# Later column starts and another split of hand-carried groups (28 / 27 / 5 in place of 29 / 28 / 4) in a graph-network layer on one Trainium2 core

## The chip, the cores and the metric

The kernel runs on one core of a Trainium2 chip. A core has five engines, each with an instruction queue of its own that runs in order: TensorE (PE, with its weight loads listed apart as PEld), VectorE (DVE), ScalarE (ACT), GpSimd (POOL) and SyncE (SP, which in this kernel issues DMAs). The engines wait for one another through semaphores only. The metric is device time in microseconds of one execution. Three runs of the kernel took 3390.92, 3395.1 and 3396.24 us, so the median is 3395.1 us.

## The reference

One layer of message passing with a gated update, over N = 12,500 nodes of 128 features and E = 400,000 edges of 32 features. The edges arrive sorted by their destination `dst`; their sources `src` are random.

```python
h = relu(layernorm(x))                                  # x is 12500 x 128
m = relu(concat(h[src], h[dst], ea) @ w1 + b1) @ w2 + b2
agg = segment_sum(m, dst, 12500)
gi, gh = agg @ w_ih + b_ih, h @ w_hh + b_hh
r = sigmoid(gi_r + gh_r);  z = sigmoid(gi_z + gh_z)
n = tanh(gi_n + r * gh_n)
out = x + (1 - z) * n + z * h
```

The costly part is `h[src]`: for each of 400,000 edges a random row of 128 floats.

## The kernel before

**Tables.** A first part computes `h` and keeps it turned round in fast memory (`hT_all`, a column of 128 features for each node). It writes to device memory A = h @ w1[0:128] (the source's part of the edge product) and B = h @ w1[128:256] + b1 (the destination's).

**Pairs and units.** The edges are 3125 tiles of 128. Eight tiles make a *pair* k (391 pairs; the first has five tiles), and half a pair is a *unit* u (782 units, k = u // 2). The main loop goes through the units. For pair k, TensorE forms the destination and edge parts of eight tiles (`pre`, line 683, weights times `L` and `RW`), VectorE adds the eight gathered rows of A and applies the relu in one instruction (`add`, line 713), and TensorE sums the result by destination (`seg`, line 739). Work is pipelined by hand: in unit u the program puts `pre` of unit u+3, `add` of unit u+2 and `seg` of unit u, so pair k's add stands in unit 2k-1. Every 14 pairs a block of nodes is finished by `node`, with gate products, activations and an output row block.

**Four ways to bring the source rows of a pair.**

- *POOL.* For most pairs GpSimd issues eight indirect DMAs (`gather`, line 163), each of which fetches 128 rows of A into one of 11 buffers `G`. The buffers are a ring: a pair takes the buffer of the pair gathered eleven pairs before it, and its first gather waits until that pair's add has read the buffer. The first nine pairs (RAW) are gathered from x itself, and their norm is computed on the spot, before A is complete.
- *ScalarE* ("act"). For some pairs ScalarE copies 1024 columns of `hT_all` one by one into `HE_act` (line 979); it reads 16 column numbers at a time into registers (line 961). TensorE multiplies them by w1a (line 694), and ScalarE applies the relu (line 725) in place of VectorE's add.
- *VectorE* ("dve"). The same on VectorE, two columns per instruction (512 instructions of line 986 a pair, and eight repacking copies of line 991), with 32 numbers per register load.
- *SyncE* ("sp"). SP issues 1024 DMAs of one row of A each (line 968) into `G_sp`, with 32 numbers per register load (line 961). VectorE then adds them as for a gathered pair. There is one `G_sp` buffer.

Such a hand-carried pair is called a group below. Which pairs are groups, and in which units an engine works on each, comes from two tables:

```python
SPREAD = {"dve": 28, "act": 29, "sp": 4}     # lines 56-57
START = {"dve": 10, "act": 2, "sp": 24}
...
for m, n in SPREAD.items():
    lo, hi = START[m] // 2 + 2, NP - {"dve": 5, "act": 3, "sp": 12}[m]
    for i in range(n):
        k = lo + int((i + 1) * (hi - lo) / n)
        while k in mode:
            k += 1
...
        end = 2 * k - (8 if m == "sp" else 4)
        jobs.setdefault(start, []).append((m, k, end - start))
        start = end if m != "sp" else 2 * k + 2
```

Each engine has a column of groups, one behind the other. A group's 1024 copies or DMAs are cut into steps (`STEP`: 4 or 8 of them) and `run_jobs` lays these steps evenly over the units from the group's start to its end, four times in each unit, between the other instructions of that engine's queue. The order is therefore fixed when the program is written; what the engines do with it in time is decided by the queues and semaphores.

**SP's queue** also carries, in the same order, the loads that all pairs need. `fetch` (lines 574 and 577) brings `L` for two pairs; it stands in unit 2k, for k even, for pairs k+6 and k+7, and waits until TensorE has read the buffer of pair k. `window_rows` (line 613) brings two row blocks `RW` of B in unit 2k for pair k+4, whose `pre` stands in unit 2k+5, five units on. At each block end come the output store (854), two stores of a new piece of B (258 and 260; the next `window_rows` waits until they have landed) and the next block's load of x (755).

**The end.** The last pair (390) is added in two halves, and `last_node` finishes the last block behind it.

Of the kernel before, what the change touches and what calls it, by code (L numbers as in the profile page):

```python
# [52 lines left out]
PIECE = 128  # L53
STEP = {"act": 4, "dve": 8, "sp": 4}
ROW = 4 * D
SPREAD = {"dve": 28, "act": 29, "sp": 4}
START = {"dve": 10, "act": 2, "sp": 24}
NR = 12672

H_AT = 16512  # L60
# [3 lines left out]
def tile_gnn(ctx: ExitStack, tc: tile.TileContext, x, src, srcT, dstT, dstP, eaT, eaP, w1, b1, w2T, b2,  # L64
# [25 lines left out]

    mode, order = {}, {m: [] for m in SPREAD}
# [3 lines that stand above are left out]
# [447 lines left out]
    def check_windows():  # L542
        m = const.tile([128, 2], F32, name="lim1")
        nc.vector.tensor_reduce(m[:, 0:1], lim[:, 0, :], AX.X, ALU.max)
        nc.vector.tensor_reduce(m[:, 1:2], lim[:, 1, :], AX.X, ALU.min)
        bad = const.tile([128, 2], F32, name="bad")
        nc.vector.tensor_scalar(bad[:, 0:1], m[:, 0:1], float(V - 1), None, op0=ALU.is_gt)
        nc.vector.tensor_scalar(bad[:, 1:2], m[:, 1:2], 0.0, None, op0=ALU.is_lt)
        one = const.tile([128, 1], F32, name="one")
        nc.vector.tensor_tensor(one, bad[:, 0:1], bad[:, 1:2], op=ALU.max)  # L550
        pm = SEGB[1][:, 384:512]
        nc.tensor.transpose(pm[0:1, :128], one, ident)
        f = const.tile([1, 8], F32, name="flags")
        nc.vector.tensor_reduce(f[:, 0:1], pm[0:1, :128], AX.X, ALU.max)
        nc.vector.tensor_reduce(f[:, 1:2], off_f, AX.XY, ALU.max)
        nc.vector.tensor_reduce(f[:, 2:3], step_f, AX.X, ALU.max)
        nc.vector.tensor_scalar(f[:, 3:4], blk_f[:, NB - 1:NB], float(N - BLOCKS[-1][2]), None,
                                op0=ALU.not_equal)
        nc.vector.tensor_copy(f[:, 4:5], beyond)
        nc.vector.tensor_reduce(f[:, 6:7], f[:, 0:5], AX.X, ALU.max)  # L560
        nc.vector.tensor_copy(flag, f[:, 6:7])
# [435 lines left out]
    for m, kl in order.items():  # L997
        start = START[m]
        for k in kl:
# [75 lines left out]
    for u in range(NU):  # L1075
        k, h = divmod(u, 2)
        gathers(u)
        if h == 0:
# [14 lines left out]
            if k == NP - 20:  # L1093
                check_windows()
        if u == min(START.values()) - 2:
            nc.vector.tensor_scalar(at[:NJ, :], at[:NJ, :], place_of[:, 0:1], place_of[:, 1:2],
# [192 lines left out]
```

## Time and profile before

| | us |
|---|---|
| median of three runs | 3395.1 |
| the profiled execution, whole | 3398.46 |
| its span, from first to last instruction | 3396.4 |

| engine | busy | what fills it |
|---|---|---|
| ACT | 3183.8 us, 94% | 29,696 column copies |
| POOL | 2536.6 us, 75% | 2637 gathers; between two of them about 0.3 us of issue, which is not counted as busy |
| PE | 2410.5 us, 71% | `pre`, `seg`, gates |
| DVE | 2254.8 us, 66% | adds, column copies; register loads in between are not counted as busy |

The granted TensorE clock was 0.795 in the mean. The profile was taken on an execution 3.4 us longer than the median. "Idle" in a row is the time in which an engine stood still just before the instructions of that row, with what ended it; "issue" means that it waited for nothing that the profile shows, which here is mostly register loads (DVE, ACT) or the engine's own overhead between two DMAs (POOL). SP's instructions never count as busy; they are seen in the order of time (the timeline) and in the waits of SP's own queue, written SPq.

### The profile page before, as it was taken

Reading aid. Unit: us, or ns where it says so; the run is one execution under the profiler, and the core shown is the slowest. Engines: PE = TensorE matmul, PEld = TensorE weight load, DVE = VectorE, ACT = ScalarE, POOL = GpSimd, SP = SyncE. Lnnn points to the kernel's source line nnn. Section 1 sums busy time; section 2 is a strip of 40 time slices with the busy share of each in tenths; the row PEclk is TensorE's granted clock in tenths of the full one; section 3 lists DMA queues with packets and bytes.
Section 4 is the critical chain, followed back from the end, with each engine's and each line's share of the span. In section 5 each row is a group of like instructions: output and inputs, shape, how many; then the busy total and the mean of one; then the engine's idle time right before and its main releaser. Section 6 shows DMA issues by size and latency. Waiting matters only on the chain. (4 is left out here: it accounts for less than half of the span.)

```text
span 3396.4 us, 92978 instructions
## 1 busy us (share of the span) xinstructions
PE 2410.5 (71%) x13145; PEld 1547.7 (46%) x13145; DVE 2254.8 (66%) x16792; ACT 3183.8 (94%) x30083; POOL 2536.6 (75%) x2646
## 2 busy tenths in 40 slices
PE   7568767776677677677767776776676577767767
PEld 7445434444444344444444443454444344444445
DVE  8566667667666676676666666666666666666665
ACT  7699999999999999899999999999998999999995
POOL 7767777777777777777777777777777777777774
PEclk9777778877878788787778778777777887778878
DMA  6333444434434444343344343443443433444432
GB/s 214 97 85 87 101 99 95 99 94 106 95 96 98 99 97 96 95 103 95 92 100 97 92 100 94 102 93 97 97 102 87 101 94 94 100 100 96 94 94 62
DMA packets 194428, 334.67 MB, mean 99 GB/s; under 512 B 68293, under 2 KB 115972, under 8 KB 193809
## 3 DMA queue, kind: packets, MB, share of 16 engines
q0 software_dynamic: 84384, 172.99, 22.8%
q1 hardware_dynamic: 109281, 155.66, 17.2%
q14 instruction: 510, 4.18, 0.4%
q8 instruction: 109, 1.79, 0.2%
q10 hardware_dynamic: 144, 0.07, 0.0%
HBM read 308.21 MB, written 20.24 MB: 97 GB/s over the span
## 5 line engine op out<-in xcount | busy, mean ns | idle before, releaser
L163 POOL DMA_INDIRECT G<-A,src_i x2568 | 2469.5, 962 | 803.0 <-issue 761.5
L979 ACT COPY HE_act<-hT_all 128x4 uint8 x29696 | 2993.9, 189 | 52.9 <-issue 27.2
L986 DVE SCALAR_TENSOR_TENSOR both<-hT_all 128x4 uint16 x14336 | 1214.1, 154 | 990.4 <-issue 980.6
L683 PE MATMUL pre<-RW,L 128*128 128x256 f32 x3128 | 1130.2, 487 | 217.0 <-DVE RB L713 200.4
L683 PEld LDWEIGHTS pre<-RW,L 128*128 128x128 f32 x3128 | 662.5, 236 | 500.2 <-DVE RB L713 216.2
L739 PE MATMUL seg<-RB,OH 128*32 128x129 f32 x6250 | 609.4, 326 | 308.1 <-DVE RB L713 238.9
L739 PEld LDWEIGHTS seg<-RB,OH 128*32 128x32 f32 x6250 | 334.8, 126 | 802.2 <-DVE RB L713 460.3
L713 DVE CUSTOM_DVE_ANT_0 RB<-pre,G 128x1024 f32<-128x1024 f32 x322 | 389.4, 1210 | 26.0 <-PE pre L683 21.6
L734 PE MATMUL seg<-zrow 1*128 1x129 bf16 x196 | 45.9, 234 | 215.0 <-DVE OH L633 212.7
L586 DVE TENSOR_SCALAR L<-L,node_of 64x512 f32<-64x512 int32 x382 | 188.7, 494 | 10.7 <-DMA L<-in_dstP 10.7
L633 DVE TENSOR_TENSOR OH<-dloc,seg 128x512 f32<-128x512 f16 (+1 forms) x198 | 132.2, 668 | 0.0
L765 PE MATMUL nd<-spot,sums 128*128 128x40 f32 x782 | 114.5, 316 | 4.8 <-DVE sums L748 4.7
L765 PEld LDWEIGHTS nd<-spot,sums 128*128 128x128 f32 x782 | 109.8, 226 | 14.4 <-issue 8.8
L991 DVE COPY HE_dve<-both 128x512 uint8<-128x512 uint8 x224 | 102.4, 457 | 7.7
L848 PE MATMUL nd<-ident,gt 128*128 128x128 f32 (+2 forms) x112 | 28.5, 400 | 98.0 <-DVE gt L844 88.0
L694 PEld LDWEIGHTS pre<-w1a,HE_act 128*128 128x128 f32 x464 | 82.0, 221 | 9.5
L244 PE MATMUL nd<-w1b,hT_all 128*128 128x128 f32 x224 | 45.5, 346 | 56.5 <-DVE xb L850 56.5
L694 PEld LDWEIGHTS pre<-w1a,HE_dve 128*128 128x128 f32 x448 | 78.8, 220 | 9.2
L163 POOL DMA_INDIRECT G<-in_x,src_i x69 | 65.7, 952 | 21.9 <-issue 20.7
L694 PE MATMUL pre<-w1a,HE_act 128*128 128x128 f32 x464 | 80.5, 302 | 0.0
L725 ACT ACTIVATE RB<-pre 128x1024 f32<-128x1024 f32 x66 | 66.8, 1013 | 13.2 <-PE pre L694 13.2
L694 PE MATMUL pre<-w1a,HE_dve 128*128 128x128 f32 x448 | 77.7, 302 | 0.0
(177 smaller groups left out, 1374.9 us busy)
## 6 DMA issues: line engine op xcount, KB each, us to landing
G_sp<-A SPq DMA_DIRECT2D x4096, 0.5 KB
L<-in_dstP SPq DMA_DIRECT2D x195, 256.0 KB
L<-in_eaP SPq DMA_DIRECT2D x195, 256.0 KB
G<-A,src_i POOLq DMA_INDIRECT x2568, 2.6
RW<-B SPq DMA_DIRECT2D x782, 16.0 KB
xb<-in_x SPq DMA_DIRECT2D x26, 256.0 KB
out<-xb SPq DMA_DIRECT2D x26, 256.0 KB
xs<-in_x SPq DMA_DIRECT2D x11, 512.0 KB
```

The costliest lines, as they stand in the source:

```text
L163: fetched = nc.gpsimd.indirect_dma_start(out=G[k][:, j, a, :], out_offset=None, in_=table, in_offset=bass.IndirectOffsetOnAxis(ap=src_i[c] ...
L586: nc.vector.tensor_scalar(o, i, node_of[:, k:k + 1], None, op0=ALU.is_equal)
L633: nc.vector.tensor_tensor(p, dloc[:, e0:e1, None].to_broadcast(shape), row[:, None, :].to_broadcast(shape), op=ALU.is_equal)
L683: nc.tensor.matmul(p[:, 2 * i:2 * i + 2, :], Ls[k // QP][:, c0:c0 + 128], RW[k % 4], start=True, stop=not raw)
L694: nc.tensor.matmul(p[:, 2 * i + a, :], cols, w1a, start=False, stop=n + 1 == len(l) or l[n + 1][1] != j)
L713: made = nc.vector._custom_dve(TENSOR_ADD_SAT, out=o, in0=p, in1=G[k].rearrange("p j a f -> p (j a) f")[:, c, :], s0=float("inf"), s1=0.0)
L725: nc.scalar.activation(o, p, AF.Relu)
L739: nc.tensor.matmul(p[r0:r0 + V, :D + 1], OH[k][:, a * GRP + j, :], RB[k % 2][:, 2 * j + a, :D + 1], start=False, stop=all(b != a for _, _, ...
L765: nc.tensor.matmul(p[:, bass.ds(offs[i], V + SHIFT)], sums[:, slot(b, i), :D], spot[:, i % 2, :], start=False, stop=i == len(offs) - 1)
L979: nc.scalar.copy(he[:, e * 4:e * 4 + 4], column(v))
L986: nc.vector.scalar_tensor_tensor(both[:, (e0 % PIECE + i) // 2, :], column(vals[i + 1]), 256.0, column(vals[i]), op0=ALU.mult, op1=ALU.add)
L991: nc.vector.tensor_copy(he[:, p0 * 4:(p0 + PIECE) * 4].rearrange("p (n c b) -> p n c b", c=2, b=4), both.bitcast(U8).rearrange("p n (b c) ...
```

## The change

```diff
-SPREAD = {"dve": 28, "act": 29, "sp": 4}
-START = {"dve": 10, "act": 2, "sp": 24}
+SPREAD = {"dve": 27, "act": 28, "sp": 5}
+START = {"dve": 14, "act": 4, "sp": 24}
```

By the formula above this gives:

| | before | after |
|---|---|---|
| groups in all | 61 | 60 |
| pairs that POOL gathers | 330 (2637 gathers) | 331 (2645 gathers) |
| ScalarE's column | 29 groups in units 2 to 772; pairs 16, 29, 42, 56 ... 374, 388 | 28 groups in units 4 to 772; pairs 17, 31, 45, 58 ... 374, 388 |
| units per ScalarE group | 26, now and then 28 | first 26, then 28, now and then 26 |
| VectorE's column | 28 groups in units 10 to 768; pairs 20, 34, 47 ... 372, 386 | 27 groups in units 14 to 768; pairs 22, 36, 50 ... 372, 386 |
| units per VectorE group | 26 and 28 by turns | first 26, then 28 |
| SP's column | 4 groups (pairs 105, 197, 287, 379) of 178, 174, 170, 174 units, in units 24 to 750 | 5 groups (pairs 87, 160, 233, 306, 379) of 142, 136, 136, 136, 136 units, in units 24 to 750 |

Between two SP groups lie ten units (five pairs) without SP rows, in both kernels. One instruction on VectorE that turns the node numbers of all groups into addresses (line 1096) moves from unit 0 to unit 2, since its place is two units ahead of the first column. Nothing else changes: the arithmetic, the ring of 11 buffers, and all other loads and their places stay.

## The prediction

> **What bounds the kernel now.** I read the page first, then the waits of POOL, then POOL's and VectorE's timelines against each other.
>
> ```profile
> span 3396.4 us, 92978 instructions
> L163 POOL DMA_INDIRECT G<-A,src_i x2568 | 2469.5, 962 | 803.0 <-issue 761.5
> L979 ACT COPY HE_act<-hT_all 128x4 uint8 x29696 | 2993.9, 189 | 52.9 <-issue 27.2
> L986 DVE SCALAR_TENSOR_TENSOR both<-hT_all 128x4 uint16 x14336 | 1214.1, 154 | 990.4 <-issue 980.6
> L991 DVE COPY HE_dve<-both 128x512 uint8<-128x512 uint8 x224 | 102.4, 457 | 7.7
> ```
>
> Three engines look full. ScalarE's copies alone take 2994 us. VectorE's column takes 1214 us of copies and 981 us of issue (register loads). POOL's gathers and their issue fill almost everything. The first question is which of them waits. From 200 us on, POOL's waits were:
>
> ```profile
> POOL G L163 <- issue: 739.3, 2422, 0.3
> POOL G L163 <- DVE RB L713: 16.4, 14, 7.7
> POOL G L163 <- DVE both L986: 8.5, 28, 0.3
> ```
> ```profile
> 400.00:3200.00 2800.00, 2125.73 (x2210) 0.79 0.41 97
> ```
>
> POOL waited for others hardly at all; from 400 to 3200 us (POOL's busy time in that window) it issued 2210 gathers in 2800 us, 1.267 us each. So it runs at its own pace, 10.1 us a pair. POOL's timeline shows where it stood still, and the last gathers of pairs 36, 376 and 390; VectorE's shows the adds of those three pairs (counted off in program order):
>
> ```profile
> 198.18 0.95 POOL L163 DMA_INDIRECT G<-A,src_i  x1 [1.72 <-PE misc L666]
> 215.62 0.95 POOL L163 DMA_INDIRECT G<-A,src_i  x1 [7.75 <-DVE RB L713]
> 316.97 0.94 POOL L163 DMA_INDIRECT G<-A,src_i  x1 [0.93 <-DVE RB L713]
> 331.02 0.94 POOL L163 DMA_INDIRECT G<-A,src_i  x1 [4.36 <-DVE RB L713]
> 350.10 0.95 POOL L163 DMA_INDIRECT G<-A,src_i  x1 [0.30 <-issue]
> 3250.00 0.95 POOL L163 DMA_INDIRECT G<-A,src_i  x1 [0.30 <-issue]
> 3361.32 0.95 POOL L163 DMA_INDIRECT G<-A,src_i  x1 [0.31 <-DMA G<-A,src_i]
> ```
> ```profile
> 445.36 1.21 DVE L713 CUSTOM_DVE_ANT_0 RB<-pre,G 128x1024 f32<-128x1024 f32 x1
> 3280.55 1.23 DVE L713 CUSTOM_DVE_ANT_0 RB<-pre,G 128x1024 f32<-128x1024 f32 x1 [0.63 <-PE pre L683]
> 3376.27 1.29 DVE L713 CUSTOM_DVE_ANT_0 RB<-pre,G 128x512 f32<-128x512 f32 x2 [3.12 <-PE pre L683]
> ```
>
> The *lag* from the end of a pair's last gather to its add is 445.36 - 351.05 = 94.3 us at pair 36, 29.6 us at 376 and 14.0 us at 390. Early on the ring is full and the consumers (VectorE, ScalarE, TensorE) hold POOL back. After 331 us POOL never waits again, and the consumers eat up the backlog: from pair 36 to 376 they take (3280.55 - 445.36) / 340 = 8.34 us a pair, while POOL needs (3250.95 - 351.05) / 340 = 8.53 us for each pair of the sequence, groups included. So the consumers set the end, but POOL is only 14 us behind as a bound. A change that frees the consumers soon runs into POOL.
>
> **The change, part by part.** (1) *One more pair for POOL.* Eight gathers at 1.267 us: +10.1 us on POOL's end. Its pace becomes 8.53 + 10.1 / 391 = 8.56 us a pair.
>
> ```profile
> L163 POOL DMA_INDIRECT G<-A,src_i x2568: 942/947/1624, 92.9 to 3361.3; - x198
> ```
>
> A rule of the Trainium skill bears on this price (SBUF — State Buffer, "Who interferes with whom"): a VectorE copy in a two-port mode locks GpSimd out of a shared port while it runs, and gathers issued by GpSimd need that port for their descriptors. By the rule, eight repacking copies of line 991 fewer, at 457 ns, could give POOL back up to 3.7 us, and the sum would be that much lower. The gather's median of 947 ns (least, median, most in the row above) and its mean of 962 leave about 40 us over all gathers for every such disturbance, so the trace allows the rule a small part only; I add nothing for it.
>
> (2) *ScalarE and VectorE have one group less.* ScalarE's copies take 2993.9 / 29696 = 0.101 us each, 103 us a group; spread over 387 pairs that frees 0.27 us a pair. On VectorE a group is (1214.1 + 980.6 + 102.4) / 28 = 82 us, or 0.21 us a pair. If they alone set the pace, the consumers come to 8.34 - 0.21 = 8.13 us a pair, well under POOL's 8.56.
>
> (3) *SP has one group more, and each is denser.* This is the part with a price.
>
> ```profile
> L968 SPq DMA_DIRECT2D G_sp<-A x4096: 224/228/760, 240.8 to 3267.5; - x196
> L961 SPq TENSOR_LOAD <-at x128: 1872/2148/2357, 238.4 to 3247.9; - x128
> ```
> ```profile
> 1119.13 3.91 SPq L968 DMA_DIRECT2D G_sp<-A  x12
> 1123.14 0.81 SPq L613 DMA_DIRECT2D RW<-B  x2
> 1124.05 6.04 SPq L968 DMA_DIRECT2D G_sp<-A  x12
> 1130.35 0.40 SPq L854 DMA_DIRECT2D out<-xb  x1
> 1132.29 0.42 SPq L258 DMA_DIRECT2D B<-xb  x1
> 1132.77 0.52 SPq L260 DMA_DIRECT2D B<-xb  x1
> 1136.60 0.90 SPq L613 DMA_DIRECT2D RW<-B  x2
> ```
> ```profile
> L968 SPq DMA_DIRECT2D G_sp<-A x840: 224/228/706, 1101.3 to 1699.4; - x168
> ```
> ```profile
> SPq L574 <- PE pre L683: 71.9, 17, 14.9
> SPq L613 <- PE pre L683: 16.0, 6, 9.1
> SPq L613 <- DMA B<-xb: 14.7, 5, 3.2
> SPq L574 <- PE pre L694: 3.7, 2, 1.9
> ```
>
> (The first two rows are the whole run's, then come a stretch of SP's timeline, the SP rows between 1100 and 1700 us, and SP's waits in those 600 us.) Twelve rows occupy SP for 1123.14 - 1119.13 = 4.01 us, 0.334 us each, and a register load adds about 2.2 us (the stretch of 6.04 us holds one): a group costs 1024 x 0.334 + 32 x 2.2 = 412 us. In the 600 us, waiting for TensorE (71.9 + 16.0 + 3.7 = 92 us) is SP's whole slack. It worked 508 us, 840 / 1024 x 412 = 338 of them on rows and 170 on everything else, landings of B included; at 8.34 us a pair that is 72 pairs, so 2.36 us a pair. After the change a group lies in 136 units, 68 pairs: 412 + 68 x 2.36 = 572 us, which is 8.42 us a pair, or, with 420 us for a group (the rows vary), 8.53. That is over the 8.13 of the other consumers and just under POOL's 8.56. SP becomes nearly full.
>
> What covers SP's lateness: `RW` is asked for five units ahead, 5 x 4.07 = 20.3 us at 8.13 us a pair. The profile has no landing time for RW; nearest is a gather's, which is
>
> ```profile
> DMA to landing us min/median/max: 2.5/2.7/5.5
> ```
>
> and at a block end SP bunches about 6 us (1130.35 to 1136.60 above). That leaves C = 20.3 - 2.7 - 6 = 12 us that SP may fall behind before TensorE waits; the bounds are 0 (a late SP costs at once) and 17 (no bunching). Between two groups SP has five pairs with little to do, 5 x (8.13 - 2.36) = 29 us, and starts anew.
>
> One cycle of 73 pairs then takes the consumers 420 + 68 x 2.36 + 5 x 8.13 - C = 621 - C, against POOL's 73 x 8.56 = 625. The lag is 94 us at pair 36, falls by 0.43 x 47 = 20 until the end of the first, longer group (pair 83), and then by 4 + C in each of four cycles: at pair 376 it is 94 - 20 - 16 - 4C, 10 us for C = 12, 58 for C = 0, nothing for C = 17. The last fifteen pairs took 29.6 - 14.0 = 15.6 us off it, and their groups are the same as before. So for C = 12 the add of the last pair waits for its rows alone, 2.7 us behind the start of the last gather, in place of 14.9: -12.2 us. For C = 0 the lag ends at 42, +28 us. I take -11, since stretches with a burst of node work leave a few us.
>
> The Trainium skill has a rule that speaks against this part (DMA: Bandwidth & Descriptors, "Rules for kernel authors" and "Anatomy of one DMA"): small transfers are mostly overhead, about 2 us fixed for each. Paid one after the other by SP, 1024 rows would be 2048 us by that page's figure, no group would fit, and the kernel would take over 10 ms. The trace disagrees on that reading: 4096 rows went out in 3027 us beside everything else. The fixed time is overlapped, and I give the rule no chance of its own here.
>
> (4) *Later starts.* POOL's four early waits above, less 0.3 us of issue each, are 1.4 + 7.45 + 0.6 + 4.1 = 13.5 us of standing still because the buffer's consumer was late. Two units without copies take 2 x 39.4 x 0.101 = 8 us out of ScalarE's queue ahead of the first two waits; but ScalarE was not full there,
>
> ```profile
> 100.00:200.00 100.00, 61.92 (x372) 50.68 (x374) 61.30 (x352) 77.29 (x509) 72.61 (x77) 0.76 0.34 85
> 200.00:300.00 100.00, 74.79 (x379) 45.49 (x378) 64.52 (x516) 99.15 (x951) 69.98 (x75) 0.76 0.34 84
> ```
>
> (the fourth busy time is ScalarE's: 77 of the first 100 us, 99 of the next), so about half of it reaches the add: 4 us. The last two waits (4.7 us) should go: by then the columns are two to four units behind, and one group (pair 17) stands before pair 21 where there were two (16 and 20), so POOL asks for that buffer one pair later. I take -8 us; bounds 0 and -13.5. A loss is excluded while SP's rows, which start in the same unit, have the cover above.
>
> VectorE's address instruction in unit 2 rather than 0 costs nothing: one instruction, still two units ahead of its reader. The two pairs that change from a ScalarE relu to a VectorE add are 1.2 us of VectorE each, inside its 82 us.
>
> *Sum:* 10.1 - 8 - 11 = -8.9 us. The profiled execution, 3398.46, becomes 3389.6; the median of the runs stands 3.4 us lower, so 3386.
>
> **The rivals.**
>
> *SP runs out of cover (the other side).* Place: TensorE's `pre`, waiting for RW or VectorE's L. Price: each us of C that is missing adds 4 us at pair 376. It decides from C under 8 us: there the end's lag is over 14 - 2.1 us and outweighs the gains. With C = 4 the lag ends at 42 - 16 = 26, +12 in place of -11: 10.1 - 8 + 12 = +14, 3409; with C = 0 it is +30, 3425. For it: 8.42 to 8.53 us a pair leaves SP almost nothing within a group, and B's landing (14.7 us in 600) can't be hidden. Against it: SP was waiting for TensorE 15% of the time, and in the whole run TensorE waited for RW in three places only:
>
> ```profile
> PE pre L683 <- DMA RW<-B: 16.6, 3, 11.3
> ```
>
> *The gains at both ends are small, and POOL's pair eats them.* The early waits stay (0) while the end still tightens: 10.1 - 11 = -1, 3394. Or the early waits go and the end's lag stays at 14 because node work, not groups, makes it: 10.1 - 8 = +2, 3397. For it: ScalarE's idle 23 us in the window with the two early waits; against it: the lag falls steadily through the run, so it is a backlog and not a fixed delay.
>
> *The consumers were all that counted* (the change does more than I allow): the end falls by VectorE's 82 us, 3313. Against it: POOL's 2645 x 1.267 us alone is 3351, with 34 us from its last gather to the span's end behind it. I give it nothing.
>
> **How the numbers follow.** Forecast 0.45; SP out of cover 0.33; small gains 0.22. The forecast's own range, from all early waits gone and C = 17 (10.1 - 13.5 - 12, -15) to C = 9 (-5), is 3380 to 3390. To reach 8 in 10 the range takes in the small gains and the rival up to about C = 2: 3379 to 3418. A difference under 0.2%, 7 us, can't be told from none here. Faster than that is the forecast; no change is the small gains; slower is SP out of cover: 0.45, 0.22, 0.33.
>
> **What would show it.** Right: POOL's waits on DVE RB after 200 us fall under 9 us; its last gather starts near 3363; the add of the last pair waits for the landing, and in the second half of the run VectorE's adds are held up by gathers rather than by TensorE. SP's waits for TensorE shrink from 92 us in 600 to some 20. Wrong: TensorE or VectorE waiting for RW or L in SP's groups, with a lag that no longer falls; POOL waiting on the ring beyond 400 us; or SP rows that cost other than 0.33 us.

## Result, and the profile after

The changed kernel takes 3381.91 us (median of five runs, 3379.55 to 3383.87), the kernel before 3396.24 us in five runs; the ratio is 0.9955, 95% interval 0.9941 to 0.9969. The forecast was 3386, with a range of its own of 3380 to 3390. The profiled execution has a span of 3382.1 us against 3396.4, so the two traces differ by 14.3 us. From the page of the changed kernel (the columns as on the page before: busy, mean ns of one, idle just before with what ended it):

```profile
span 3382.1 us, 93395 instructions
...
L163 POOL DMA_INDIRECT G<-A,src_i x2576 | 2475.8, 961 | 790.4 <-issue 761.2
L979 ACT COPY HE_act<-hT_all 128x4 uint8 x28672 | 2889.0, 189 | 52.9 <-issue 29.1
L986 DVE SCALAR_TENSOR_TENSOR both<-hT_all 128x4 uint16 x13824 | 1174.3, 154 | 930.3 <-issue 925.6
L683 PE MATMUL pre<-RW,L 128*128 128x256 f32 x3128 | 1136.1, 489 | 461.3 <-DMA RW<-B 237.7
...
L713 DVE CUSTOM_DVE_ANT_0 RB<-pre,G 128x1024 f32<-128x1024 f32 x323 | 391.1, 1211 | 70.9 <-DMA G<-A,src_i 56.5
```

Two of these rows read quite differently from before. TensorE's `pre` now waits 238 us for RW, which SP brings (before: 16.6). VectorE's add now waits for gathered rows, 56.5 us (before: not at all). The second is the mark of POOL as the bound. POOL's waits from 200 us on, its last gathers of pairs 37, 261, 370, 376 and 390 (36 is a VectorE group now, so 37 stands for it), and the adds of the same pairs:

```profile
POOL G L163 <- issue: 738.0, 2420, 0.3
POOL G L163 <- DVE both L986: 7.6, 25, 0.3
POOL G L163 <- DVE RB L713: 5.2, 17, 0.3
```
```profile
345.79 0.94 POOL L163 DMA_INDIRECT G<-A,src_i  x1 [0.30 <-issue]
...
2261.59 0.95 POOL L163 DMA_INDIRECT G<-A,src_i  x1 [0.30 <-issue]
...
3203.85 0.94 POOL L163 DMA_INDIRECT G<-A,src_i  x1 [0.30 <-issue]
...
3244.44 0.95 POOL L163 DMA_INDIRECT G<-A,src_i  x1 [0.31 <-issue]
...
3354.97 0.94 POOL L163 DMA_INDIRECT G<-A,src_i  x1 [0.30 <-issue]
```
```profile
441.81 1.21 DVE L713 CUSTOM_DVE_ANT_0 RB<-pre,G 128x1024 f32<-128x1024 f32 x1
...
2272.34 1.21 DVE L713 CUSTOM_DVE_ANT_0 RB<-pre,G 128x1024 f32<-128x1024 f32 x1
...
3210.39 1.22 DVE L713 CUSTOM_DVE_ANT_0 RB<-pre,G 128x1024 f32<-128x1024 f32 x1
...
3265.06 1.23 DVE L713 CUSTOM_DVE_ANT_0 RB<-pre,G 128x1024 f32<-128x1024 f32 x1 [0.33 <-PE pre L683]
...
3361.10 1.29 DVE L713 CUSTOM_DVE_ANT_0 RB<-pre,G 128x512 f32<-128x512 f32 x2 [3.15 <-PE pre L683]
```

No wait of POOL on a buffer is longer than its usual 0.3 us any more: the early waits are gone. The lag is 95 us at pair 37 (before: 94 at pair 36), 10 at 261, 6 at 370, 20 at 376 and 5 at 390. So the consumers have eaten up the backlog by pair 261 (before they never did), then wait for POOL pair by pair, fall behind once more over the last thirty pairs, where groups and node blocks lie close, and are 5 us late at the end. From pair 376 to the last add they take 96.0 us, before it was 95.7.

The 14.3 us are therefore: POOL's last gather starts at 3354.97 instead of 3361.32 (-6.3, made of ten us for the pair that was added, -13.5 for the early waits, and -3 for slightly shorter gathers and a shorter wait at 125 us), the lag of the last pair falls from 14.0 to 5.2 (-8.8), and what follows the last add takes 21.0 instead of 20.1 (+0.9).

SP is nearly full inside a group. Its rows in the whole run, and its waits for others from 880 to 1430 us, all within the second group:

```profile
L968 SPq DMA_DIRECT2D G_sp<-A x5120: 224/228/912, 229.4 to 3253.7; - x197
```
```profile
SPq L613 <- DMA B<-xb: 12.7, 5, 3.3
SPq L574 <- PE pre L694: 0.9, 2, 0.5
...
SPq L574 <- PE pre L683: 0.4, 1, 0.4
...
SPq L613 <- PE pre L683: 0.2, 1, 0.2
```

In 550 us it waited 2.1 us for TensorE (two entries left out here, of 0.4 and 0.2 us, belong to it). That group's rows took 564 us (868.9 to 1433.3) for 68 pairs, 8.30 us a pair; the third group's took 575 us (1456.7 to 2031.6), 8.45 a pair.

### The profile page after: what moved, and what is told of

Read it like the earlier page. It is cut to its first block, busy times and chain, and to the rows that moved or that the text cites. A ratio compares the mean times of both kernels' runs of the same rounds, so it can differ in the third digit from the quotient of the medians.

```text
span 3382.1 us, 93395 instructions
## 1 busy us (share of the span) xinstructions
PE 2400.4 (71%) x13113; PEld 1554.8 (46%) x13113; DVE 2213.6 (65%) x16274; ACT 3081.1 (91%) x29057; POOL 2542.8 (75%) x2654
## 5 line engine op out<-in xcount | busy, mean ns | idle before, releaser
L979 ACT COPY HE_act<-hT_all 128x4 uint8 x28672 | 2889.0, 189 | 52.9 <-issue 29.1
L986 DVE SCALAR_TENSOR_TENSOR both<-hT_all 128x4 uint16 x13824 | 1174.3, 154 | 930.3 <-issue 925.6
L739 PE MATMUL seg<-RB,OH 128*32 128x129 f32 x6250 | 592.7, 319 | 244.2 <-DVE RB L713 211.9
L739 PEld LDWEIGHTS seg<-RB,OH 128*32 128x32 f32 x6250 | 328.0, 123 | 590.7 <-DVE RB L713 310.1
L713 DVE CUSTOM_DVE_ANT_0 RB<-pre,G 128x1024 f32<-128x1024 f32 x323 | 391.1, 1211 | 70.9 <-DMA G<-A,src_i 56.5
L586 DVE TENSOR_SCALAR L<-L,node_of 64x512 f32<-64x512 int32 x382 | 185.9, 487 | 62.2 <-DMA L<-in_dstP 59.9
L694 PEld LDWEIGHTS pre<-w1a,HE_dve 128*128 128x128 f32 x432 | 89.1, 255 | 12.4
L694 PE MATMUL pre<-w1a,HE_dve 128*128 128x128 f32 x432 | 85.4, 333 | 0.0
L244 PEld LDWEIGHTS nd<-w1b,hT_all 128*128 128x128 f32 x224 | 35.2, 231 | 85.5 <-DVE xb L850 80.0
```

The source lines that it names most:

```text
L244: nc.tensor.matmul(pm[:m, i:i + D], hT_all[:, n0 + i:n0 + i + m], w1b, start=True, stop=True)
L586: nc.vector.tensor_scalar(o, i, node_of[:, k:k + 1], None, op0=ALU.is_equal)
L694: nc.tensor.matmul(p[:, 2 * i + a, :], cols, w1a, start=False, stop=n + 1 == len(l) or l[n + 1][1] != j)
L713: made = nc.vector._custom_dve(TENSOR_ADD_SAT, out=o, in0=p, in1=G[k].rearrange("p j a f -> p (j a) f")[:, c, :], s0=float("inf"), s1=0.0)
L739: nc.tensor.matmul(p[r0:r0 + V, :D + 1], OH[k][:, a * GRP + j, :], RB[k % 2][:, 2 * j + a, :D + 1], start=False, stop=all(b != a for _, _, ...
L979: nc.scalar.copy(he[:, e * 4:e * 4 + 4], column(v))
```

## Experiments

Each run was timed beside the kernel before on its chip; ratios are to that. The whole change has 0.9955. Beside the whole change and the first eight runs, the kernel before had medians of 3396.24, 3397.57 and 3401.64 us, so a difference of a few us between the medians of two runs is better read from their ratios. The theory at the start: the consumers set the end before, POOL sets it after, and POOL's early waits count in full; the rivals put the gain into one part of the change or see the crowded SP queue as a cost.

**The later starts alone.**

```diff
 SPREAD = {"dve": 28, "act": 29, "sp": 4}
-START = {"dve": 10, "act": 2, "sp": 24}
+START = {"dve": 14, "act": 4, "sp": 24}
```

> The later starts alone (ScalarE from unit 4, VectorE from unit 14), with the old split of 29, 28 and 4 groups. Theory: POOL's early waits of 13.5 us go, so its last gather starts near 3346 instead of 3361, but ScalarE and VectorE still carry 61 groups' worth of work between them, so the consumers end where they ended and the lag at the last pair grows from 14 us to 25 or more: 3392 to 3400 us, no change from before. Rival (the early waits of POOL alone make the gain): 3382 to 3385 us, as with the whole change.

Measured: ratio 1.0016 (1.0004 to 1.0028), median 3405.12 beside 3397.57, so no gain, and 5 us above the upper end of what was expected. The end of its trace, last gather and last adds:

```profile
3346.39 0.94 POOL L163 DMA_INDIRECT G<-A,src_i  x1 [0.30 <-issue]
...
3384.43 1.29 DVE L713 CUSTOM_DVE_ANT_0 RB<-pre,G 128x512 f32<-128x512 f32 x2 [3.14 <-PE pre L683]
```

POOL is done 15 us earlier, as forecast, and the last pair's add comes 37 us behind it, 8 us later than before the change. POOL's early waits are worth nothing by themselves. The add of pair 36 stands 9 us earlier than before the change, but from there to pair 376 the consumers took 8.39 us a pair against 8.34, and lost it again; why isn't settled.

**The new split alone.**

```diff
-SPREAD = {"dve": 28, "act": 29, "sp": 4}
+SPREAD = {"dve": 27, "act": 28, "sp": 5}
 START = {"dve": 10, "act": 2, "sp": 24}
```

> The new split alone (28, 27 and 5 groups), with the old starts in units 2 and 10. Theory: POOL carries one pair more (+10 us), most of its early waits stay (8 to 13 us of standing still after 190 us), and the consumers still come within 5 us of the last gather (-8): 3390 to 3397 us, which is 8 to 15 us over the whole change. Rival (the relief of ScalarE and VectorE makes the gain, the starts do nothing): 3380 to 3384 us.

Measured: 0.9955 (0.9939 to 0.9970), median 3384.40: the whole gain. The rival was right. Its early waits, last gather and last two half adds:

```profile
196.16 0.94 POOL L163 DMA_INDIRECT G<-A,src_i  x1 [2.78 <-PE misc L666]
...
213.39 0.94 POOL L163 DMA_INDIRECT G<-A,src_i  x1 [7.53 <-DVE RB L713]
...
3361.17 0.94 POOL L163 DMA_INDIRECT G<-A,src_i  x1 [0.30 <-DMA G<-A,src_i]
```
```profile
3361.46 0.69 DVE L713 CUSTOM_DVE_ANT_0 RB<-pre,G 128x512 f32<-128x512 f32 x1 [3.21 <-PE pre L683]
...
3363.91 0.69 DVE L713 CUSTOM_DVE_ANT_0 RB<-pre,G 128x512 f32<-128x512 f32 x1 [1.76 <-DMA G<-A,src_i]
```

The early waits stayed (9.7 us beyond the usual; before the change it was 13.5). POOL ended when it had ended before the change (3361.17 against 3361.32), although it carried a pair more: its waits of every kind were 6 us shorter, and its gathers were 0.960 us long in the mean instead of 0.961, some 3 us in all. That is 6 us later than in the whole change, and the first half of the last pair was added at the same time, 3361. Here the consumers were right behind POOL: the second half waited for its rows. In the whole change they were 5 us late. So POOL's earlier end gave the consumers nothing; each of the two is within a few us of being the bound at the end. Why the consumers took 4 us less from pair 370 to 376 here (50.4 against 54.7 us) isn't settled; the granted clock was 0.803 in this profile and 0.795 in the other.

**Four SP groups in the changed kernel**, so one pair more for POOL.

```diff
-SPREAD = {"dve": 27, "act": 28, "sp": 5}
+SPREAD = {"dve": 27, "act": 28, "sp": 4}
```

> The changed kernel with four SP groups in place of five, so 59 groups and 332 pairs for POOL. Theory (POOL sets the end of the changed kernel; SP's fullness costs nothing there): 8 gathers more, +10 us, 3390 to 3395 us, while TensorE's waits for RW fall from 226 us to under 40. Rival (the crowded SP queue costs the changed kernel time): same or faster than 3382 us.

Measured: 0.9976 (0.9965 to 0.9987), median 3390.01, span 3392.1. TensorE's waits for RW after 200 us fell from 226 to 8 us, the backlog was gone by pair 140 instead of 261 (7.87 us a pair from 37 to 140, against 8.17), and yet the kernel was 10 us longer in its span, 8 in its median (by the ratios, 7). TensorE's waits for RW in the whole change and here, from 200 us on, then the add of pair 140 in the whole change, the adds of pairs 37 and 140 here, and the end here:

```profile
PE pre L683 <- DMA RW<-B: 226.0, 65, 9.4
```
```profile
PE pre L683 <- DMA RW<-B: 8.2, 2, 5.3
```
```profile
1283.38 1.22 DVE L713 CUSTOM_DVE_ANT_0 RB<-pre,G 128x1024 f32<-128x1024 f32 x1
```
```profile
436.48 1.21 DVE L713 CUSTOM_DVE_ANT_0 RB<-pre,G 128x1024 f32<-128x1024 f32 x1
...
1246.74 1.23 DVE L713 CUSTOM_DVE_ANT_0 RB<-pre,G 128x1024 f32<-128x1024 f32 x1 [1.98 <-DMA G<-A,src_i]
...
3367.96 0.94 POOL L163 DMA_INDIRECT G<-A,src_i  x1 [0.30 <-issue]
...
3372.31 1.29 DVE L713 CUSTOM_DVE_ANT_0 RB<-pre,G 128x512 f32<-128x512 f32 x2 [3.01 <-PE pre L683]
```

POOL's last gather starts 13 us later, ten of them for the added pair and most of the rest for longer gathers (0.962 us in the mean). So POOL is the bound of the changed kernel, a pair costs it about its 10 us, and the crowded SP queue slows the consumers while they have a backlog and costs nothing at the end.

**Six RW buffers in the changed kernel**, asked for two pairs earlier.

```diff
-            nc.sync.dma_start(RW[k % 4].bitcast(U8)[V * a:V * (a + 1), a, :],
+            nc.sync.dma_start(RW[k % 6].bitcast(U8)[V * a:V * (a + 1), a, :],
...
-            window_rows(k + 4)
+            window_rows(k + 6)
```

> The changed kernel with six RW buffers in place of four, asked for seven units ahead of use plus two more (window rows of pair k+6 in place of k+4 in unit 2k), so that a late SP has four more units of cover. Theory (the waits for RW lie on the way only while the backlog is eaten, POOL sets the end): TensorE's 226 us of waits for RW fall under 60, the lag reaches its floor at an earlier pair, and the time stays at 3378 to 3385 us. Rival (SP's lateness sets the pace): 3350 to 3372 us.

Measured: 0.9948 (0.9931 to 0.9966), median 3380.55. TensorE no longer waited for RW at all after 200 us, and the time stayed. But the lag did not reach its floor sooner: 60.8, 57.9 and 7.3 us at pairs 84, 121 and 261, against 62.7, 58.3 and 9.8. The 226 us of TensorE's waits were not what slowed the consumers. SP is as full as before in this run, and VectorE still waits 40.5 us for `L`, the other load that SP brings. Those waits in the whole change and here, from 200 us on:

```profile
DVE L L586 <- DMA L<-in_dstP: 50.2, 21, 5.9
```
```profile
DVE L L586 <- DMA L<-in_dstP: 40.5, 18, 6.4
```

Between 440 and 1285 us, about the stretch of pairs 37 to 140, they are 28.1 us in the whole change, 23.1 us here, and none with four SP groups, where these pairs took 31.3 us less than in the whole change (810.3 against 841.6). So the sizes fit a late SP that holds up VectorE through `L`. No run asks for `L` earlier, so this stays argued and not shown.

**Six SP groups.**

```diff
-SPREAD = {"dve": 27, "act": 28, "sp": 5}
+SPREAD = {"dve": 27, "act": 28, "sp": 6}
```

> The changed kernel with six SP groups (61 groups, 330 pairs for POOL), each in 110 to 116 units. Theory (SP's queue is full within its five groups, so a sixth makes it the bound of the whole run): a group costs SP 419 us and the rest 2.2 to 2.4 us a pair, which is 6 x 419 + 363 x 2.3 = 3350 us of SP work between units 24 and 750, beside some 25 us of empty time in each of five gaps; with 230 us ahead and 125 us behind, 3750 to 3830 us, POOL waiting on its ring to the end. Rival (a late SP is hidden by its cover): within 15 us of 3382.

Measured: 1.0932 (1.0906 to 1.0959), median 3717.54, from two executions. TensorE's waits, VectorE's and POOL's:

```profile
PE pre L683 <- DMA RW<-B: 917.4, 176, 11.5
```
```profile
DVE L L586 <- DMA L<-in_dstP: 407.9, 110, 11.8
```
```profile
POOL G L163 <- DVE RB L713: 291.8, 77, 17.9
```

SP's rows took 529 to 558 us a group, each group denser than its time allows; the lag stayed at 85 to 123 us from pair 15 to 387, which is the full ring. VectorE waited 348 us more for `L` than in the whole change (59.9 over its whole run), and the span is 332 us longer; the sizes are near again. This is the forecast's rival, SP out of cover, one group further on. The reckoning was 1 to 3% too long.

**VectorE back at 28 groups, and ScalarE back at 29**, each in the changed kernel, each with one pair less for POOL.

```diff
-SPREAD = {"dve": 27, "act": 28, "sp": 5}
+SPREAD = {"dve": 28, "act": 28, "sp": 5}
```

> The changed kernel with VectorE back at 28 groups (28, 28 and 5; 61 groups, 330 pairs for POOL). Theory: POOL has 8 gathers less (-10 us) and, with the later starts, its last gather starts near 3345, but VectorE is as full as before the change and sets the pace again, so the lag at pair 376 stays over 30 us: 3385 to 3400 us. Rival (only ScalarE was too full): 3370 to 3376 us, faster than the whole change.

```diff
-SPREAD = {"dve": 27, "act": 28, "sp": 5}
+SPREAD = {"dve": 27, "act": 29, "sp": 5}
```

> The changed kernel with ScalarE back at 29 groups (27 for VectorE, 5 for SP; 61 groups, 330 pairs for POOL). Theory: ScalarE sets the pace again, lag at pair 376 over 30 us, 3385 to 3400 us. Rival (only VectorE was too full): 3370 to 3376 us.

Measured: with VectorE at 28, 1.0047 (1.0030 to 1.0064), median 3417.24; with ScalarE at 29, 0.9923 (0.9907 to 0.9938), median 3373.79. The last gather and last adds of the first, and then of the second:

```profile
3344.16 0.94 POOL L163 DMA_INDIRECT G<-A,src_i  x1 [0.30 <-issue]
...
3386.51 1.29 DVE L713 CUSTOM_DVE_ANT_0 RB<-pre,G 128x512 f32<-128x512 f32 x2 [3.12 <-PE pre L683]
```
```profile
3345.68 0.94 POOL L163 DMA_INDIRECT G<-A,src_i  x1 [0.30 <-DMA G<-A,src_i]
...
3351.89 1.29 DVE L713 CUSTOM_DVE_ANT_0 RB<-pre,G 128x512 f32<-128x512 f32 x2 [3.14 <-PE pre L683]
```

POOL ends alike in both. With the VectorE group the consumers need 8.42 us a pair from 37 to 261 and end 41 us behind POOL; with the ScalarE group they need 8.16, as in the whole change, and end 5 us behind. The theory was right for VectorE in kind, though the time came out above its 3385 to 3400 us, and wrong for ScalarE, where the rival was right: ScalarE, busy 94% of the time with 29 groups, still kept up. Taking the ScalarE group away, as the change does, only hands POOL a pair: the run with 29 is 0.3% faster than the whole change and beats both kernels.

**Columns that end earlier** in the changed kernel.

```diff
-        lo, hi = START[m] // 2 + 2, NP - {"dve": 5, "act": 3, "sp": 12}[m]
+        lo, hi = START[m] // 2 + 2, NP - {"dve": 10, "act": 8, "sp": 12}[m]
```

> The changed kernel with ScalarE's and VectorE's columns ending ten units earlier (last groups 383 and 381 in place of 388 and 386). Theory (in the changed kernel the last twenty pairs are paced by the groups and node blocks there, so that the last pair's add stands 5 us behind its rows although POOL had been the bound before): with fewer groups at the end the lag at the last pair falls to 2 us or less, and the time to 3375 to 3381 us. Rival (POOL's last gather alone sets the end): the same as the whole change, 3382, whatever the lag.

Measured: 0.9925 (0.9910 to 0.9940), median 3374.54, as the theory had it within half a us, and not the rival's 3382. Its last gather, and the two halves of its last add:

```profile
3349.66 0.94 POOL L163 DMA_INDIRECT G<-A,src_i  x1 [0.30 <-DMA G<-A,src_i]
```
```profile
3347.32 0.69 DVE L713 CUSTOM_DVE_ANT_0 RB<-pre,G 128x512 f32<-128x512 f32 x1 [3.17 <-DMA G<-A,src_i]
...
3352.31 0.69 DVE L713 CUSTOM_DVE_ANT_0 RB<-pre,G 128x512 f32<-128x512 f32 x1 [4.30 <-DMA G<-A,src_i]
```

The lag at the last pair is gone: the first half is added before the last gather, and the second waits for its rows. The span is 12.4 us shorter than that of the whole change. Of these, 5.3 us are not the edit's aim: POOL ended that much sooner with the same number of gathers, because they were 0.959 us long in the mean instead of 0.961; why isn't known. The other 7.1 us lie behind the last gather. So the 5 us that the whole change left at its end go when the groups there go.

**Four runs on a chip that behaved otherwise.** They were to isolate one engine's group against the kernel before, and to add up the two gains.

```diff
 the kernel before, VectorE alone:   SPREAD = {"dve": 27, "act": 29, "sp": 4}
 the kernel before, ScalarE alone:   SPREAD = {"dve": 28, "act": 28, "sp": 4}
 changed, columns ending earlier:    SPREAD = {"dve": 27, "act": 29, "sp": 5}
 changed, columns ending earlier:    SPREAD = {"dve": 26, "act": 30, "sp": 5}
```

> The kernel before, with one VectorE group taken away and nothing else (29, 27 and 4; starts in units 2 and 10): 60 groups, 331 pairs for POOL, as in the whole change. Theory (VectorE was the engine that set the pace before; everything else in the change is beside the point): 3379 to 3388 us, as the whole change. Rival (ScalarE's or SP's share of the change is needed too): 3392 to 3400 us.

> The kernel before, with one ScalarE group taken away and nothing else (28, 28 and 4; starts in units 2 and 10): 60 groups, 331 pairs for POOL. Theory (VectorE sets the pace, with 28 groups as before): no gain, 3395 to 3412 us, with a lag at pair 376 of 20 us or more. Rival (any group less will do): 3379 to 3388 us.

> The changed kernel with 29 ScalarE groups (61 groups, 330 pairs for POOL) and both columns ending ten units earlier. Theory (the two gains of the runs with these edits add up, since POOL sets the end in both): 10 us from POOL's pair and 5 to 8 us from the end, 3362 to 3369 us. Rival (with columns this dense ScalarE or SP falls behind): 3372 to 3385 us.

> As the run before, with one more group moved from VectorE to ScalarE (30, 26 and 5; 61 groups). Theory (ScalarE at 30 groups is full, since a group took it 106 us at the least, 30 x 106 = 3180 us of the 3200 us between its first column and the last): ScalarE sets the pace, slower than the run with 29, 3370 to 3390 us. Rival (ScalarE still has room): 3360 to 3367 us.

Measured: on this chip the kernel before itself took 5755.64 us (twelve runs, 5722.98 to 5769.26), 1.7 times its time elsewhere. The four had 1.0150 (1.0126 to 1.0174), 0.9937 (0.9913 to 0.9960), 1.0141 (1.0121 to 1.0160) and 1.0330 (1.0311 to 1.0348). From the first one's trace:

```profile
L979 ACT COPY HE_act<-hT_all 128x4 uint8 x29696 | 3279.1, 192 | 2180.2 <-issue 2153.7
L163 POOL DMA_INDIRECT G<-A,src_i x2576 | 2469.4, 959 | 3158.7 <-DVE RB L713 2285.3
```
```profile
DVE both L986 <- issue: 1636.4, 1671, 2.8
```

ScalarE's copies were as long as ever one by one, but ScalarE stood still for 2154 us in between, waiting for nothing that the profile shows; VectorE had more such gaps too (1636 us), and POOL waited 2285 us on its ring. ScalarE's copies and the gaps before them fill 5459 of the 5827 us, so it was probably the bound here. Among the four the ratios rise with its groups (0.9937 with 28, 1.0141 and 1.0150 with 29, 1.0330 with 30), but the kernel before has 29 groups too, at a ratio of 1, so its groups alone don't explain them. None of the four expectations could be put to the test: the ratios say nothing about the balance on the other chips. Whether one VectorE group less is enough in the kernel before, and whether the two gains add up, stays open.

## Why the prediction was right, and where not

*What bounds the kernel.* Right. The consumers set the end before (the starts alone moved POOL's end by 15 us and gained nothing), POOL sets the pace from pair 261 on after the change, and an added pair of POOL costs about 10 us (four SP groups).

*POOL's pair, +10.1.* Right: +10 in the span with four SP groups; the last gather 9.3 us earlier with ScalarE back at 29.

*The relief of ScalarE and VectorE.* The size came from VectorE, 0.21 us a pair, and that is the engine that counted: its one group is worth 0.25 us a pair, and with it back the last add stands 34.6 us later than with ScalarE's group back (3386.51 against 3351.89). ScalarE's relief, which the prediction set beside it, was not needed.

*SP.* Nearly full, as reckoned: its waits for TensorE shrank to 2.1 us in 550, and two groups took 8.30 and 8.45 us a pair, where 8.42 to 8.53 was written. The step that failed here is the cover C. It was worked out from RW alone, and each us of it was to be worth four at the end. Six RW buffers add four units to it, which is 16 us at the prediction's 4.07 us a unit; TensorE's waits for RW were gone, and the backlog fell no faster. The rival named VectorE's `L` beside RW, but the reckoning of C left `L` out, and it is VectorE's waits for `L` whose size fits what a full SP costs (argued, see six RW buffers). SP did slow the consumers (8.17 against 7.87 us a pair with four groups), and still the backlog went faster than reckoned: the reckoning has lags of 74, 58, 42 and 26 us behind the first four groups, the trace 63, 47, 18 and 11 (pairs 84, 157, 229 and 303). The forecast lag at pair 376, 10 us, was 20, since a new lag arises near the end, which the reckoning by whole cycles can't see.

*The end, -11.* In size near: -8.8 at the last add and +0.9 behind it. The last add did not come to wait for its rows alone, as the forecast had it: it started 6.1 us behind the start of the last gather, where 2.7 was written.

*The later starts, -8.* Failed as a term of the sum. The waits went altogether, -13.5 us, more than taken, and POOL's end moved with them. But the new split alone, with the early waits in place, gave the whole gain. What stood in their place is the lag at the end, which was 5.2 us with the later starts and about nothing without: the two terms share one end, and a sum that gives each its own size counts them twice. The two runs have the same ratio, 0.9955; their medians differ by 2.5 us, which lies within their scatter.

*The sum.* -8.9 forecast, -14.3 in the trace: 5.5 us more from POOL's early waits than taken and 3 us more from its shorter gathers, 3 us less at the end. That the forecast of the time came so near is in part luck. Without the starts its terms are 10.1 - 11 = -0.9, and the run without the starts gained as much as the whole: there the consumers came up to POOL altogether (-14.7 at the last add), and POOL's shorter waits and gathers took back the pair that it carried more.

*The rivals.* SP out of cover did not come with five groups and came in full with six. Of the small gains, one half was true: at the end of the changed kernel node work and groups do hold 5 us, and ending the columns earlier takes them back.

## What to carry to other kernels

Where several engines look full, the lag between producer and consumer, followed from the start to the end of the run, can tell which one sets the end. Here a lag that shrank through the whole run meant that the consumers set it, one that lay at its floor meant POOL, and the stalls of POOL while it was ahead cost nothing. Busy shares didn't rank the full ones: ScalarE carried 29 groups at 94% and kept up; VectorE with 28, at 66% and with 981 us of issue, mostly register loads, in between, did not. When work is handed from full engines to the one that will be the bound, hand over only what the slowest of them can't carry.

## What the runs showed of the hardware

On one chip the kernel before took 5755.64 us in place of some 3397. The durations of copies (192 ns against 189) and gathers (959 against 962) were as elsewhere; what was new were gaps between instructions, in the first of the four runs 2154 us of them between ScalarE's copies in 3025 places, none longer than 1.9 us, and 1636 us before VectorE's column copies, where the whole change had 926. The granted TensorE clock was 0.667 there, against 0.795 in the profiles of the kernel before and of the whole change elsewhere:

```profile
ACT HE_act L979 <- issue: 2153.7, 3025, 1.9
```

The runs don't show what held the instructions up.
